# A Macaron block on one core: FFN and Mamba cut into steps and woven by a written order

## The chip, the cores and the metric

The kernel runs on one core of a Trainium2 chip. The metric is the device time of one execution in microseconds. The core has engines that each work through a queue of their own, in order: TensorE (PE, matrix products), VectorE (DVE, elementwise and scans), ScalarE (ACT, activation functions, each from a table that must be loaded), GpSimd (POOL), and SyncE (SP), which here issues the transfers (DMA). An engine waits for another by semaphores.

## The reference, cut to what matters

Four sequences of 512 tokens and 128 features pass through two Macaron blocks. The first is half an FFN, a Mamba layer, half an FFN; the second is half a mixture of experts, attention, half a mixture of experts. The change concerns the first one:

```python
# FFN on layernorm(x), 128 -> 512 -> 512 -> 512 -> 128
h = silu(x @ w1) * (x @ w2)
h = gelu(h @ h1)
h = gelu(h @ h2)
return h @ w3
# Mamba on layernorm(x); 256 inner channels, 16 states
x_ssm, z = split(x @ in_proj)
xc = silu(causal_conv(x_ssm, 4 taps) + conv_b)
dt_r, B, C = split(xc @ x_proj)              # 1, 16, 16 columns
dt = softplus(dt_r @ dt_proj + dt_proj_b)
h_t = exp(dt * A) * h_(t-1) + dt * B * xc    # for every channel and state
y = sum_n(h * C) + xc * D
return y * silu(z) @ out_proj
# x = x + FFN(x)/2;  x = x + Mamba(x);  x = x + FFN(x)/2
```

All is computed in float32.

## The kernel before, in words

Activations lie with the features across the 128 partitions and the 512 tokens of a sequence (here called a block, 0 to 3; x0 to x3) along a row. `first_half` treats the first Macaron block, `second_half` the mixture of experts and attention.

`ffn` makes two 512 wide products into one PSUM tile `pair` (two buffers). The first layer has 8 matmuls, a Silu (L244) and a gate product (L245); each of the two hidden layers has 16 matmuls (L227) in two halves with a Gelu after each half (L251); the last has 4 (L255) and an add into x (L257).

`mamba_first` is everything ahead of the scan: layernorm (L186 to L202), the products with in_w (L271, L276), the convolution on VectorE (L281, L283), Silu, the row of dt apart from the rows of B and C (L291, L293), dt's softplus from Exp and Ln (L319 to L330). B and C go to DRAM and come back broadcast over 32 partitions each (L300, L306), in a pool of three buffers. `mamba_spread` (L337) copies 32 channels of dt and of dt*xc four times over the partitions: tile `rep`, four of them per block, k = 0 to 3.

The scan of a block has 16 steps, 8 in each of two halves. A step is two Exps that make `da` (L349, three buffers), a product with B (L351), two scans (L353) and a product with C (L354) on VectorE, and two narrow matmuls that sum over states into `acc` (L361). `mamba_last` adds the skip term (L371), makes y (L375), multiplies by out_w (L379) and adds into x (L380).

In `first_half` FFN 0 and `mamba_first` of block 0 come first. Then for each block: the first half of the scan, one FFN (in block 0 FFN 1 ahead of the scan and FFN 2 and 3 in the middle; later the second FFN of the block before), `mamba_first` of the next block, the second half of the scan, `mamba_last`. The second FFN of block 3 comes after all this, beside the first routing of the experts.

This text is not the order on the engines. A scheduler at build time puts every instruction into its engine's queue by the order of the text, by its own estimates of durations and by priority: what stands under `with early()` counts as standing 3000 places ahead. In the queue the order is then fixed. `wait_for` makes an instruction wait for another's end, `ln_exp` loads a table once an instruction is done.

Of the kernel before, what the change touches and what calls it, by code (L numbers as in the profile page):

```python
# [29 lines left out]
P = 128  # L30
# [13 lines left out]
EARLY = 3000  # L44
EPS = 1e-5
# [10 lines left out]
def macaron(ctx: ExitStack, tc: tile.TileContext, a: dict, out: bass.AP):  # L56
# [161 lines left out]
    def ffn(pool, pair, b):  # L218


        def product(w, h, c, n):

            ps = pair.tile([P, 2, S], F32, tag="pair", name="pair")
            for i in range(2):
                cut = slice((2 * c + i) * P, (2 * c + i + 1) * P)
                for k in range(n):
                    nc.tensor.matmul(  # L227
                        ps[:, i, :],
                        lhsT=w[:, cut] if n == 1 else w[:, k, cut],
                        rhs=h if n == 1 else h[:, k, :],  # L230
                        start=k == 0,
                        stop=k == n - 1,
                    )
            return ps

        with early():
            xn = layernorm(b)
        h = pool.tile([P, NH, S], F32, tag="h", name="h")
        for c in range(NH // 2):
            p1 = product(w1, xn, c, 1)  # L240
            p2 = product(w2, xn, c, 1)
            g = pool.tile([P, 2, S], F32, tag="g", name="g", bufs=1)
            with early():
                nc.scalar.activation(g, p1, AF.Silu)  # L244
                nc.vector.tensor_mul(h[:, 2 * c : 2 * c + 2, :], p2, g)  # L245
        for w in (h1, h2):
            nxt = pool.tile([P, NH, S], F32, tag="h", name="hn")
            for c in range(NH // 2):
                ps = product(w, h, c, NH)
                with early():  # L250
                    nc.scalar.activation(nxt[:, 2 * c : 2 * c + 2, :], ps, AF.Gelu)  # L251
            h = nxt
        ps = pair.tile([P, 2, S], F32, tag="pair", name="pair")[:, 0, :]
        for k in range(NH):
            nc.tensor.matmul(ps, lhsT=w3[:, k, :], rhs=h[:, k, :], start=k == 0, stop=k == NH - 1)  # L255
        with early():
            nc.vector.tensor_add(xs[b], ps, xs[b])  # L257

# [3 lines left out]
    def mamba_first(pool, b):  # L262
        with early():
            xn = layernorm(b)
        xi = pool.tile([P, NC, S + DCONV - 1], F32, tag="xi", name="xi", bufs=1)
        nc.gpsimd.memset(xi[:, :, 0 : DCONV - 1], 0.0)
        z = pool.tile([P, NC, S], F32, tag="z", name="z")
        for c in range(NC):
            ps = aux()
            with early():  # L270
                nc.tensor.matmul(ps, lhsT=in_w[:, c * P : (c + 1) * P], rhs=xn, start=True, stop=True)  # L271
            nc.scalar.copy(xi[:, c, DCONV - 1 :], ps)
        for c in range(NC):
            ps = aux()
            with early():
                nc.tensor.matmul(ps, lhsT=in_w[:, DI + c * P : DI + (c + 1) * P], rhs=xn, start=True, stop=True)  # L276
            nc.scalar.activation(z[:, c, :], ps, AF.Silu)
        xc = pool.tile([P, NC, S], F32, tag="xc", name="xc")
        for c in range(NC):
            cv = pool.tile([P, S], F32, tag="cv", name="cv")  # L280
            nc.vector.tensor_scalar_mul(cv, xi[:, c, 0:S], col(V_CW + c * DCONV))  # L281
            for k in range(1, DCONV):
                nc.vector.scalar_tensor_tensor(  # L283
                    cv, xi[:, c, k : k + S], col(V_CW + c * DCONV + k), cv, ALU.mult, ALU.add
                )
            nc.scalar.activation(xc[:, c, :], cv, AF.Silu, bias=col(V_CB + c))
        ps_r = aux(1)
        ps_bc = aux(2 * NST)
        with early():
            for k in range(NC):  # L290
                nc.tensor.matmul(ps_r, lhsT=xp_w[:, k, 0:1], rhs=xc[:, k, :], start=k == 0, stop=k == NC - 1)  # L291
            for k in range(NC):
                nc.tensor.matmul(ps_bc, lhsT=xp_w[:, k, 1:], rhs=xc[:, k, :], start=k == 0, stop=k == NC - 1)  # L293
        rank = pool.tile([1, S], F32, tag="rank", name="rank", bufs=1)
        nc.scalar.copy(rank, ps_r)
        bc = pool.tile([2 * NST, S], F32, tag="bc", name="bc", bufs=1)
        nc.scalar.copy(bc, ps_bc)

        rows = dram.tile([2 * NST, S], F32, tag="rows", name="rows")
        nc.sync.dma_start(out=rows, in_=bc)  # L300
        bcs = []
        for i, name in enumerate(("B", "C")):
            t = pool.tile([P, NQ, S], F32, tag="bcs", name=name, bufs=3)
            for m in range(NM):
# [3 lines left out]
                    in_=rows[lo : lo + NQ].rearrange("q t -> (q t)").partition_broadcast(R),  # L308
                )
            bcs.append(t)  # L310

        both = pool.tile([P, 2, NC, S], F32, tag="both", name="both", bufs=1)
        dt, dx = both[:, 0], both[:, 1]
        e = pool.tile([P, NC, S], F32, tag="e", name="e", bufs=1)
        for c in range(NC):
            ps = aux()
            with early():
                last = nc.tensor.matmul(ps, lhsT=dt_w[:, c * P : (c + 1) * P], rhs=rank, start=True, stop=True)
            nc.scalar.activation(e[:, c, :], ps, AF.Abs, bias=col(V_DTB + c))  # L319
            nc.scalar.activation(dt[:, c, :], ps, AF.Relu, bias=col(V_DTB + c))  # L320
        u = pool.tile([P, NC, S], F32, tag="u", name="u", bufs=1)
        table = ln_exp(last)
        first = nc.scalar.activation(e, e, AF.Exp, scale=-1.0)
        after(table, first)
        nc.scalar.activation(dx, e, AF.Ln, bias=1.0)
        nc.vector.tensor_scalar(u, e, 1.0, 1.0, ALU.add, ALU.subtract)
        nc.vector.tensor_sub(u, e, u)
        nc.vector.tensor_add(u, u, dx)
        nc.vector.tensor_add(dt, dt, u)
        nc.vector.tensor_mul(dx, dt, xc)  # L330
        return z, xc, bcs, both

    def mamba_spread(pool, both, k):

        t = pool.tile([P, 2, NC, S], F32, tag="rep", name="rep", bufs=4)
        for m in range(NM):
            nc.sync.dma_start(out=t[m * R : (m + 1) * R], in_=both[k * R : (k + 1) * R])  # L337
        return t

    def mamba_half(pool, made, ys, half):  # L340
        z, xc, (bs, cs), both = made
        ks = (2 * half, 2 * half + 1)
        reps = [mamba_spread(pool, both, k) for k in ks]
        for q in range(NQ):
            sums = []
            for k, t in zip(ks, reps):
                da = pool.tile([P, NC, S], F32, tag="da", name="da", bufs=3)
                for c in range(NC):
                    nc.scalar.activation(da[:, c, :], t[:, 0, c, :], AF.Exp, scale=neg_a[:, k, c, q : q + 1])  # L349
                h = pool.tile([P, NC, S], F32, tag="hs", name="hs", bufs=4)  # L350
                nc.vector.tensor_mul(h, t[:, 1], bs[:, q].unsqueeze(1).to_broadcast([P, NC, S]))  # L351
                for c in range(NC):
                    nc.vector.tensor_tensor_scan(h[:, c, :], da[:, c, :], h[:, c, :], 0.0, ALU.mult, ALU.add)  # L353
                nc.vector.tensor_mul(h, h, cs[:, q].unsqueeze(1).to_broadcast([P, NC, S]))  # L354
                sums.append((k, h))

            with early():
                for k, h in sums:
                    for c in range(NC):
                        at = (k + 2 * c) % 4 * R  # L360
                        nc.tensor.matmul(  # L361
                            ys[c][at : at + R, :], lhsT=sum4, rhs=h[:, c, :], start=q == 0, stop=False,
                            skip_group_check=True,
                        )

    def mamba_last(pool, b, made, ys):
        z, xc, _, _ = made
        y = pool.tile([P, NC, S], F32, tag="e", name="y", bufs=1)
# [5 lines left out]
        for c in range(NC):  # L374
            nc.vector.tensor_mul(y[:, c, :], z[:, c, :], ys[c])  # L375
        with early():
# [3 lines left out]
        nc.vector.tensor_add(xs[b], xs[b], ps)  # L380

    def first_half(fpool, pair):


        with tc.tile_pool(name="mamba", bufs=2) as pool:
            ffn(fpool, pair, 0)
            made = mamba_first(pool, 0)
            for b in range(NB):
                now = made
                if b == 0:  # L390
                    ffn(fpool, pair, 1)
                ys = [acc() for _ in range(NC)]
                mamba_half(pool, now, ys, 0)
                if b == 0:
                    ffn(fpool, pair, 2)
                    ffn(fpool, pair, 3)
                else:
                    ffn(fpool, pair, b - 1)
                if b + 1 < NB:
                    made = mamba_first(pool, b + 1)  # L400
                mamba_half(pool, now, ys, 1)
                mamba_last(pool, b, now, ys)
# [401 lines left out]
```

## Time and profile before

| | us |
|---|---|
| median of 3 runs | 1862.45 (1861.93 to 1862.87) |
| profiled execution | 1863.84 |
| its span, first to last instruction | 1862.1 |
| first half, to x3 out of Mamba | 0 to 564.2 |
| last FFN, experts and attention | 564.2 to 1862 |
| TensorE busy in the whole span | 1737.3 |
| VectorE busy in the whole span | 1122.8 |
| ScalarE busy in the whole span | 814.8 |
| mean granted clock of TensorE | 0.972 |

The page cuts the span into 40 slices of 46.6 us; each digit is the busy share in tenths. A row of a stage table gives, for a stretch of the span, the busy time of each engine with the number of its instructions, the granted clock of TensorE (1.00 is full speed), the busy share of the transfer engines and what they moved. A row of waits reads: engine, what it was about to do and its line, what it waited for, us in total, how many times, the longest. A row of the timeline reads: start, length, engine, line, operation, what it writes and reads, how many in sequence, and in brackets the idle time ahead of it and what ended that. A float32 matmul is recorded as two passes, so x32 are 16 matmuls.

### The profile page before, as it was taken

How to read it: one execution, taken by the hardware profiler on the slowest of the kernel's cores; microseconds unless marked ns; L12 is line 12 of the kernel's file. 1: busy time of each engine (PE TensorE's matmuls, PEld its weight loads, DVE VectorE, ACT ScalarE, POOL GpSimd, SP SyncE). 2: the span in 40 equal slices, each digit the busy share in tenths (PEclk: the TensorE clock that was granted, in tenths of full speed). 3: DMA queues.
4: the chain of work that ended last, by engine and by line, in shares of the span. 5: the costliest groups of instructions: out<-in, count | busy, mean ns of one | idle time of the engine just before them, and what ended most of it. 6: DMA issues, size and time to landing. Idle time of an engine off the chain costs nothing.

```text
span 1862.1 us, 13356 instructions
## 1 busy us (share of the span) xinstructions
PE 1737.3 (93%) x4482; PEld 753.0 (40%) x4482; DVE 1122.8 (60%) x1976; ACT 814.8 (44%) x1213; POOL 4.3 (0%) x22
## 2 busy tenths in 40 slices
PE   6899999795949999999999999999999999999999
PEld 3333333231303444444455445544454445444443
DVE  3138969796793555656466556655665566565554
ACT  2357867483623322323444445443544355422222
POOL 0000000000000000000000000000000000000000
PEclk9989999996959999999999999999999999999999
DMA  2060232305006000000000000000000000000000
GB/s 95 5 133 0 59 78 58 79 10 127 1 0 227 1 1 0 0 0 1 0 1 0 1 1 0 1 0 0 1 1 6 1 1 0 6 1 1 6 1 6
DMA packets 14442, 42.28 MB, mean 23 GB/s; under 512 B 5068, under 2 KB 6053, under 8 KB 11045
## 3 DMA queue, kind: packets, MB, share of 16 engines
q1 hardware_dynamic: 14373, 41.43, 8.9%
q8 instruction: 35, 0.57, 0.1%
q14 instruction: 34, 0.28, 0.0%
HBM read 23.33 MB, written 1.31 MB: 13 GB/s over the span
## 4 chain that ended last, share of the span: by engine, by line
PE 72%; DVE 18%; ACT 6%; issue 3%; DMA 1%; SPq 0%; DVEq 0%; ACTq 0%
PE acc L514 16%; PE pair L519 15%; PE pair L520 15%; DVE hs L353 7%; PE pair L227 7%; PE aux L575 4%; PE acc L613 4%; DVE hs L351 3%; DVE hs L354 2%; PE aux L603 2%; PE aux L195 2%; PE aux L560 1%; PE aux L567 1%; ACT L160 1%; PE aux L189 1%
## 5 line engine op out<-in xcount | busy, mean ns | idle before, releaser
L522 ACT ACTIVATE g<-pair 128x512 f32<-128x512 f32 (+1 forms) x368 | 219.7, 597 | 639.6 <-PE pair L520 638.3
L525 DVE TENSOR_TENSOR gr<-g,rw 128x512 f32<-128x512 f32 x352 | 242.7, 690 | 338.7 <-ACT g L522 338.7
L514 PE MATMUL acc<-h,wd 128*128 128x512 f32 x704 | 362.4, 596 | 8.7 <-DVE h L528 8.7
L519 PE MATMUL pair<-xn,wg 128*128 128x512 f32 x704 | 359.9, 593 | 0.0
L520 PE MATMUL pair<-xn,wu 128*128 128x512 f32 x704 | 359.5, 592 | 0.0
L528 DVE TENSOR_TENSOR h<-gr,pair 128x512 f32<-128x512 f32 x352 | 240.5, 686 | 25.4 <-DVE gr L525 0.9
L514 PEld LDWEIGHTS acc<-h,wd 128*128 128x128 f32 x704 | 128.8, 189 | 175.9 <-DVE h L528 110.7
L520 PEld LDWEIGHTS pair<-xn,wu 128*128 128x128 f32 x704 | 133.4, 190 | 161.4 <-issue 158.8
L519 PEld LDWEIGHTS pair<-xn,wg 128*128 128x128 f32 x704 | 126.3, 190 | 119.9 <-issue 117.2
L353 DVE TENSOR_TENSOR_SCAN hs<-da,hs 128x512 f32<-128x512 f32 x128 | 150.0, 1209 | 29.0 <-ACT da L349 28.8
L361 PE MATMUL acc<-hs,sum 128*32 128x512 f32 x256 | 84.5, 697 | 62.8 <-DVE hs L354 62.8
L227 PE MATMUL pair<-h,h 128*128 128x512 f32 x256 | 117.3, 602 | 2.4 <-ACT g L244 2.3
L227 PE MATMUL pair<-hn,h 128*128 128x512 f32 x256 | 117.5, 601 | 0.0
L349 ACT ACTIVATE da<-rep,neg_a 128x512 f32<-128x512 f32 x128 | 83.9, 712 | 39.2 <-DVE hs L353 38.8
L575 PE MATMUL aux<-kt,q 128*128 128x512 f32 (+3 forms) x256 | 91.4, 441 | 4.1 <-ACT pt L608 2.7
L588 ACT ACTIVATE p<-p,a_low 128x128 f32<-128x128 f32 (+3 forms) x128 | 70.2, 549 | 31.6 <-DVE a_low L577 31.6
L354 DVE TENSOR_TENSOR hs<-hs,C 128x1024 f32<-128x1024 f32 x64 | 77.7, 1214 | 0.2
L351 DVE TENSOR_TENSOR hs<-rep,B 128x1024 f32<-128x1024 f32 x64 | 76.5, 1206 | 1.2 <-PE acc L361 1.2
L613 PE MATMUL acc<-pt,vo 128*128 128x512 f32 (+3 forms) x256 | 76.2, 433 | 0.0
L227 PEld LDWEIGHTS pair<-h,h 128*128 128x128 f32 x256 | 46.6, 190 | 72.2 <-issue 61.4
L227 PEld LDWEIGHTS pair<-hn,h 128*128 128x128 f32 x256 | 46.7, 190 | 69.4 <-issue 65.7
L577 DVE CUSTOM_DVE_ANT_0 p<-aux,mask 128x512 f32<-128x512 f32 (+3 forms) x128 | 62.0, 487 | 21.0 <-PE aux L575 21.0
(149 smaller groups left out, 1504.2 us busy)
## 6 DMA issues: line engine op xcount, KB each, us to landing
rep<-both SPq DMA_DIRECT2D x64, 256.0 KB, 7.3
B<-rows SPq DMA_DIRECT2D x16, 256.0 KB, 4.7
C<-rows SPq DMA_DIRECT2D x16, 256.0 KB, 4.9
h<-in_h SPq DMA_DIRECT2D x2, 1024.0 KB, 9.0
wg<-in_wg SPq DMA_DIRECT2D x4, 384.0 KB, 7.4
wu<-in_wu SPq DMA_DIRECT2D x4, 384.0 KB, 7.4
wd<-in_wd SPq DMA_DIRECT2D x4, 384.0 KB, 7.4
wg<-in_wg SPq DMA_DIRECT2D x4, 320.0 KB, 7.2
```

Source lines behind the costliest of these rows:

```text
L227: nc.tensor.matmul(ps[:, i, :], lhsT=w[:, cut] if n == 1 else w[:, k, cut], rhs=h if n == 1 else h[:, k, :], start=k == 0, stop=k == n - 1,)
L351: nc.vector.tensor_mul(h, t[:, 1], bs[:, q].unsqueeze(1).to_broadcast([P, NC, S]))
L353: nc.vector.tensor_tensor_scan(h[:, c, :], da[:, c, :], h[:, c, :], 0.0, ALU.mult, ALU.add)
L354: nc.vector.tensor_mul(h, h, cs[:, q].unsqueeze(1).to_broadcast([P, NC, S]))
L514: nc.tensor.matmul(po, lhsT=w, rhs=h, start=n == 0, stop=n == len(jobs) - 1)
L519: nc.tensor.matmul(pg, lhsT=wg_, rhs=xn, start=True, stop=True)
L520: nc.tensor.matmul(pu, lhsT=wu_, rhs=xn, start=True, stop=True)
L522: nc.scalar.activation(g, pg, AF.Silu)
L525: nc.vector.tensor_mul(gr, g, rw)
L528: nc.vector.tensor_mul(h, g, pu)
L575: nc.tensor.matmul(sc, lhsT=q[:, i * P : n], rhs=kt[:, 0:n], start=True, stop=True)
L613: nc.tensor.matmul(po[:, j * P :], lhsT=vo[:, j, h, :], rhs=pt[:, lo : lo + n], start=h == 0 and j == 0, stop=h == HEADS - 1 and j == NT - ...
```

## The change

`ffn`, `mamba_first` and the scan become generators that stop after each step: an FFN has 12 steps, `mamba_first` 6, a scan 16 and its end. `first_half` asks for one step after another: FFN 0 with the first step of FFN 1 in it; `mamba_first` of block 0 with two steps of FFN 1 after each of its own; then, in each block, after every scan step as many FFN steps as `FILL` says, and from the fifth scan step on, at every second one, a step of the next block's `mamba_first`. In block 0 these are the rest of FFN 1, and FFN 2 and 3; in blocks 1 to 3 three FFN steps follow three of every four scan steps (the second FFN of the block before).

The tiles rep 0 and 1 of the next block are now filled before the last part of a block, and B and C have four buffers, so that those of two blocks fit. Both Gelus of a layer run one after the other, and the first waits for the last matmul of the layer. dt's row and the rows of B and C come out of one matmul with 33 columns. All of `mamba_first` and the sums and end of a block stand under `early()`. Some tiles share memory under common names (`inner`, `wide`).

```diff
+FILL = ((2, 1) * 7 + (1, 1), *[(0, 1, 1, 1) * 4] * 3)
 def ffn(pool, pair, b):
...
         with early():
             xn = layernorm(b)
+        yield
...
         for w in (h1, h2):
             nxt = pool.tile([P, NH, S], F32, tag="h", name="hn")
+            both = [two(), two()]
             for c in range(NH // 2):
-                ps = product(w, h, c, NH)
-                with early():
-                    nc.scalar.activation(nxt[:, 2 * c : 2 * c + 2, :], ps, AF.Gelu)
+                product(both[c], 0, w, h, c, NH)
+                yield
+                last = product(both[c], 1, w, h, c, NH)
+                if c:
+                    with early():
+                        for i in range(2):
+                            act = nc.scalar.activation(nxt[:, 2 * i : 2 * i + 2, :], both[i], AF.Gelu)
+                            if not i:
+                                wait_for(last, act)
+                yield
...
 def mamba_first
-                nc.tensor.matmul(ps_r, lhsT=xp_w[:, k, 0:1], rhs=xc[:, k, :], start=k == 0, stop=k == NC - 1)
-            for k in range(NC):
-                nc.tensor.matmul(ps_bc, lhsT=xp_w[:, k, 1:], rhs=xc[:, k, :], start=k == 0, stop=k == NC - 1)
+                nc.tensor.matmul(ps, lhsT=xp_w[:, k, :], rhs=xc[:, k, :], start=k == 0, stop=k == NC - 1)
+            nc.scalar.copy(rows, ps)
...
-            t = pool.tile([P, NQ, S], F32, tag="bcs", name=name, bufs=3)
+            t = pool.tile([P, NQ, S], F32, tag="bcs", name=name, bufs=4)
...
 def first_half
-            ffn(fpool, pair, 0)
-            made = mamba_first(pool, 0)
...
+            STEPS = 12
+            order = [f for b in range(1, NB) for f in [before_[b]] * STEPS]
+            second = [ffn(fpool, pair, b) for b in range(NB - 1)]
+            order += [f for f in second for _ in range(STEPS)]
...
+            go(before_[0], 4)
+            filler(1)
+            go(before_[0], STEPS - 4)
+            first = mamba_first(pool, 0, made)
+            for _ in first:
+                filler(2)
             for b in range(NB):
-                now = made
+                rest = mamba_rest(pool, b, made)
                 if b == 0:
-                    ffn(fpool, pair, 1)
-                ys = [acc() for _ in range(NC)]
-                mamba_half(pool, now, ys, 0)
...
+                    mamba_spread(pool, 0, made, 0)
+                    mamba_spread(pool, 0, made, 1)
+                mamba_spread(pool, b, made, 2)
+                mamba_spread(pool, b, made, 3)
+                nxt = mamba_first(pool, b + 1, made) if b + 1 < NB else iter(())
+                for step in range(4 * NQ):
+                    go(rest)
+                    if step >= 4 and step % 2 == 0:
+                        go(nxt)
+                    filler(FILL[b][step])
                 if b + 1 < NB:
-                    made = mamba_first(pool, b + 1)
-                mamba_half(pool, now, ys, 1)
-                mamba_last(pool, b, now, ys)
+                    mamba_spread(pool, b + 1, made, 0)
+                    mamba_spread(pool, b + 1, made, 1)
+                go(rest)
```

## The prediction

> **What bounds the kernel now.** I read the page first, then a table of busy time by stage, then the waits of VectorE, then single stretches of the timeline.
>
> ```profile
> span 1862.1 us, 13356 instructions
> PE 1737.3 (93%) x4482; PEld 753.0 (40%) x4482; DVE 1122.8 (60%) x1976; ACT 814.8 (44%) x1213; POOL 4.3 (0%) x22
> ...
> PE   6899999795949999999999999999999999999999
> ...
> DVE  3138969796793555656466556655665566565554
> ...
> PEclk9989999996959999999999999999999999999999
> ```
>
> The averages mislead: from slice 14 on (the second half, which the change does not touch) TensorE is full. The digits below 9 lie in the first 12 slices, and there VectorE is the one at 9.
>
> ```profile
> core 0: us, PE busy (x) PEld busy (x) DVE busy (x) ACT busy (x) POOL busy (x), PEclk, DMA share, GB/s
> 70.00:153.00 83.00, 70.96 (x146) 27.48 (x146) 30.09 (x35) 44.53 (x51) 0.10 (x1) 0.88 0.37 77
> 153.00:244.00 91.00, 82.81 (x205) 26.61 (x203) 80.83 (x78) 67.09 (x77) 0.10 (x1) 1.00 0.27 57
> 244.00:353.00 109.00, 98.12 (x237) 32.33 (x236) 93.54 (x92) 72.29 (x85) 0.10 (x1) 0.97 0.30 63
> 353.00:455.00 102.00, 79.42 (x188) 23.88 (x188) 86.36 (x85) 65.20 (x77) 0.00 (x0) 0.90 0.23 50
> 455.00:564.20 109.20, 75.75 (x164) 22.04 (x164) 79.46 (x73) 43.23 (x52) 0.57 (x2) 0.77 0.09 19
> 564.20:1862.00 1297.80, 1274.35 (x3420) 594.10 (x3420) 737.02 (x1585) 506.41 (x856) 2.38 (x8) 1.00 0.03 9
> ```
>
> The cuts are the moments at which Mamba has finished a block (x0 at 244, x1 at 353, x2 at 455, x3 at 564.2). Everything after 564.2 hangs on x3 and takes 1297.8. So the question is when x3 is ready. VectorE is idle 15.5, 15.6 and 29.7 us in the last three blocks, TensorE more, ScalarE most: VectorE's queue sets the pace, with holes. From the first steady scans at 158.6 to its last C product's end at 554.8 it is busy 334.3 of 396.2 us, idle 61.9. What it waits for there:
>
> ```profile
> DVE xn L201 <- ACT rs L199: 15.0, 6, 5.5
> DVE y L375 <- PE acc L371: 12.1, 6, 4.0
> DVE h L245 <- PE pair L227: 10.2, 3, 6.1
> DVE xm L191 <- PE aux L189: 9.1, 5, 2.7
> DVE hs L353 <- ACT da L349: 8.5, 3, 3.9
> ```
>
> The first four are the seam between two blocks: sums, y, out_w, layernorm, gate of the next FFN, one after another with no scan to put between. Why there is none shows in SP's queue:
>
> ```profile
> 222.54 0.51 SPq L337 DMA_DIRECT2D rep<-both  x1
> 225.88 1.69 SPq L306 DMA_DIRECT2D C<-rows  x4
> 227.62 17.33 SPq L337 DMA_DIRECT2D rep<-both  x15
> ```
>
> C of block 1 stood until a third buffer came free at block 0's last B product, and 15 rep transfers stood behind it.
>
> **The steady price.** Without disturbance a step (B product, two scans, C product) takes 4.50 us of VectorE:
>
> ```profile
> 519.74 2.33 DVE L353 TENSOR_TENSOR_SCAN hs<-da,hs 128x512 f32<-128x512 f32 x2
> 519.87 1.92 PE L361 MATMUL acc<-hs,sum 128*32 128x512 f32 x4 [4.05 <-DVE hs L354]
> ...
> 524.24 2.33 DVE L353 TENSOR_TENSOR_SCAN hs<-da,hs 128x512 f32<-128x512 f32 x2
> ```
>
> that is 1.13 an instruction when they follow each other. A 512 wide matmul is 0.86 (16 of them from 113.12 to 126.96).
>
> **The change, in stages.** I laid the recorded order of the new program, queue by queue, over these durations.
>
> *To x0 (FFN 0).* The layernorm of x1 moves into FFN 0: 2 matmuls, +1.7. Both Gelus of a layer now wait for its last matmul, so TensorE stands while the first runs: about 0.2 + 1.02 + 0.1, 1.35 a layer, twice. x0 at 75 against 70.75.
>
> *To x1.* TensorE does FFN 1 (44 matmuls), in_w 4, xp 2, dt 2, two layernorms 4: 56 x 0.86 = 48. The waits inside Mamba's first part (its convolution, the two aux buffers, which copies free) I put at 4, the Gelu waits at 2.7: x1 at 129, before 146.2 (17 earlier, since mamba_first(0) no longer runs on a standing TensorE). B and C in one matmul with dt's row: 2 matmuls and a 0.57 copy fewer per block; the slack that TensorE and ScalarE have in every later stage hides it, and at the start it is inside the 48.
>
> *To steady scans.* Here it loses again. mamba_first(1) is now asked for from step 4, and stands in ScalarE's queue ahead of the da that scans 2 and 3 need. From x1 ScalarE's queue holds 12 table loads (15.4) and 25 activations (17), with some 6 of waits: steady scans at 168, two steps and six B products done. Before: 158.6.
>
> *To the y of block 0.* VectorE's queue from there: 30 scans, 11 B and 15 C products at 1.13 (63), u and dt of block 1 5.5, two gates 2.3, one add 0.6: 72, with the first step of block 1 in it. 241; before 239.4. TensorE needs some 65 in it and does not bind.
>
> *Blocks 1 to 3.* VectorE's work by count: 87 + 90 + 78.5 = 255.6. Its waits: at seam 0/1 a scan stands between the last sum and y, so y waits for nothing; what stays is out_w (1.2), the mean (1.2), the second mean (1.6), 2 for da. 6 in all. At seam 1/2 no scan stands there in the new order: y 4.5, 1.2, 1.2, then the gate of the next FFN (4 matmuls, Silu's table load, Silu) 5.7, and 2 where the dx of block 3 waits behind a pair of Gelus: 14.6. At seam 2/3 one B product lies before y and two scans before out_w: 3.5, mean 0.7, layernorm's table load, Ln and Exp 5.5, gate 1.8: 11.5. Together 32, where before some 56 of waiting lay between the y of block 0 and 554.8. Last C product's end: 241 + 255.6 + 32 = 528.6. From there 9.4 to x3, as 554.8 to 564.2: x3 at 538, **26.2 earlier**.
>
> *The rest.* In the last FFN nothing is woven in, so 2 x 1.35 of Gelu waits appear; the new order puts four transposes (0.6) and one layernorm (1.7), which before stood after it, into these waits: +0.4. Transfers: bufs 4 for B and C let C go at once; rep 0 and 1 of the next block are issued at half a block. A block's rep takes 17.3 to 18.9 us of issue, and the first half it serves lasts 8 x 4.5 = 36, so that they cost nothing; were this cover gone, one rep would be 5 to 7 us at a seam. The rows, B and C of the block after next stand in SP's queue behind rep 2 and 3, which wait for buffers that come free at a block's end; the rows are made only some five steps later. The shared names `inner` and `wide` order xi, e and y, and cv and u, one after another, as the computation does anyhow: nothing. Sum on the span: -25.8. The profiled execution itself was 1863.84, 1.7 above its span, and the median of the runs 1862.45; I take the difference over to it: **1837**.
>
> **Two rules against rows.** (1) The row: through the lonely scans of block 3 (516 to 552) the granted clock is 0.54 and a pair of sums takes 1.92, with pauses of only 2.58 us; the same pair in the full stretch takes 1.05. The Trainium skill ("TensorE: Matmul & The Clock Gate", "Why this matters for your kernels") says that only pauses over some 3 us throttle. It bears on this change, which spreads TensorE's work thinner: the new order still ends block 2 with six sums and block 3 with three with nothing between. By the rule these seams would be warm, y about 2 us sooner at each, x3 at 534; by the row they are as cold as before. I take the row. Where three matmuls lie between sums, TensorE has 3.5 of 4.5 us to do and both say warm. (2) The same skill's "ScalarE: Activation LUTs" ("What ACT_TABLE_LOAD costs") asks 2.66 us for a switch, drain included; here the load at 472.32 is followed by its da at 473.61, 1.29 later. The new order has 82 loads where there were 101 before the second half's first sigmoid: 24 us of ScalarE by the row, 51 by the rule. It was busy at most 72 of 109, so neither is on the path; but by the rule the 12 loads ahead of the steady scans would cost 17 more, and x3 would come at 555.
>
> **Rivals.** *The weave fills more* (I took the order of the queues as strict at every place where two of them meet): the gate waits, the da and dx waits and half the y waits go, 17 us; 1820. For it: within a block VectorE already ran 46.0 of 46 us at 280 to 326. Against: layernorm and out_w are true chains, and the new order leaves them bare at two seams.
> *The start costs more*: if mamba_first(1) holds steady scans back to 180 rather than 168, 12 of 26 are gone: 1849. For it: the two queues wait for each other there (da behind Silu behind convolution behind scans).
> *Slower: a pair of Gelus at the head of ScalarE's queue.* It now waits for the whole layer, and the da of the next scans stand behind it. 12 pairs lie in the woven stretch; da has three buffers, so a pair that waits up to two steps (9 us) is hidden. In block 3 before, single Gelus that waited 5.9 and 2.5 cost VectorE 3.9 and 3.4 us. At 3.9 a pair it is 47, less the 2 counted: 1882; it decides from 28 / 12 = 2.3 us a pair. Against: the new order puts 10 to 13 da ahead of most pairs.
> *The change does not reach the end*: the transfers were not late, and block 0 ends no earlier; with the waits of the old seams kept, the start's loss of 1.6 and the Gelu waits leave 1862 to 1865.
>
> **How the numbers follow.** My account 0.58 (own range 1825 to 1848, from +-12 on 32 of waits and on the 168); fills more 0.17; start costs more 0.16; no effect 0.04; slower 0.05. 0.2% is 3.7 us, about what a measurement of this kernel can tell from no change. Faster 0.91, same 0.04, slower 0.05. No waits at all in blocks 1 to 3 would be 1805; I cut the range at 1815 below, and above at 1857, where the start has lost 20 of the 26.
>
> **What would show it.** x1 added at 129 and x0 at 75; VectorE steady only from about 168; the y of block 0 near 241; x0, x1, x2 out of Mamba near 244, 338, 446 and x3 at 538; waits of VectorE from the first steady scan to its last C product about half of 61.9; y waiting for nothing at the first seam and 4 at the second; 1298 after x3. I am wrong if scans wait for da for more than 10 us in all, or if x3 comes after 556.

## The result, and the profile after

The changed kernel takes 1835.53 us (median, 1834.04 to 1835.65) against 1862.19 of the kernel before: a ratio of 0.9855, 95% interval 0.9838 to 0.9873. The prediction was 1837, range 1815 to 1857. The profiled execution took 1834.04, its span is 1832.2. It is the fastest of its kernel's four, and the profiled one of the kernel before (1863.84) is above all its other runs; so the two spans differ by 29.9 where the medians differ by 26.7, and a difference of some 3 us between two profiles is not yet an effect.

From the page of the changed kernel: the busy times, and the rows of TensorE, VectorE and the granted clock in 40 slices.

```profile
PE 1717.3 (94%) x4466; PEld 749.4 (41%) x4466; DVE 1123.2 (61%) x1976; ACT 785.3 (43%) x1189; POOL 4.3 (0%) x22
PE   6999899785869999999999999999999999999999
DVE  3127989798963656556566646665566466565554
PEclk9999999997989999999999999999999999999999
```

VectorE does the same work as before (1123 us, 1976 instructions). ScalarE lost 29 us and 24 instructions, most of it table loads; it was never full, and an experiment below gives the loads back. What changed is how tightly VectorE's work lies. The table by stages from x0 on, cut where a block has left Mamba:

```profile
core 0: us, PE busy (x) PEld busy (x) DVE busy (x) ACT busy (x) POOL busy (x), PEclk, DMA share, GB/s
244.65:341.34 96.69, 83.50 (x202) 27.01 (x200) 86.27 (x84) 60.71 (x74) 0.11 (x1) 0.96 0.32 66
341.34:446.75 105.41, 79.77 (x184) 24.66 (x184) 93.13 (x91) 60.34 (x74) 0.00 (x0) 0.87 0.29 61
446.75:532.90 86.15, 66.25 (x164) 20.82 (x164) 75.30 (x69) 39.12 (x48) 0.49 (x2) 0.94 0.00 0
532.90:1832.20 1299.30, 1274.51 (x3420) 594.13 (x3420) 737.08 (x1586) 504.55 (x855) 2.46 (x9) 1.00 0.03 9
```

Blocks 1 to 3 take 96.7, 105.4 and 86.2 us where they took 109.3, 102.1 and 108.7 (from one add into x to the next). The gain of 31 up to x3 (564.2 to 532.9) is made in block 1 (13) and above all in block 3 (23); block 2 is 3 longer, x0 comes 0.6 later, and the part after x3 is 1.5 longer. VectorE's waits from the y of block 0 to the last C product:

```profile
DVE y L394 <- PE acc L390: 7.9, 4, 3.8
DVE h L249 <- ACT g L248: 7.0, 1, 7.0
DVE xn L202 <- ACT rs L200: 4.5, 1, 4.5
DVE xm L192 <- PE aux L190: 4.2, 3, 1.6
```

With four small rows they are 29.3 us. All that these four show lies at the three seams. What feeds a scan hardly appears: in the whole answer no B product or scan waits for a transfer or for `da`.

### The profile page after: what moved, and what is told of

Read it like the earlier page. It is cut to its first block, busy times and chain, and to the rows that moved or that the text cites. A ratio compares the mean times of both kernels' runs of the same rounds, so it can differ in the third digit from the quotient of the medians.

```text
span 1832.2 us, 13288 instructions
## 1 busy us (share of the span) xinstructions
PE 1717.3 (94%) x4466; PEld 749.4 (41%) x4466; DVE 1123.2 (61%) x1976; ACT 785.3 (43%) x1189; POOL 4.3 (0%) x22
## 4 chain that ended last, share of the span: by engine, by line
PE 72%; DVE 17%; ACT 7%; issue 3%; DMA 0%; SPq 0%; DVEq 0%; ACTq 0%
PE acc L559 16%; PE pair L565 16%; PE pair L564 16%; DVE hs L376 7%; PE pair L225 6%; PE aux L620 4%; PE acc L658 4%; DVE hs L374 3%; DVE hs L377 2%; PE aux L648 2%; PE aux L605 2%; PE aux L612 2%; PE aux L196 1%; PE aux L190 1%; PE pair L268 1%
## 5 line engine op out<-in xcount | busy, mean ns | idle before, releaser
L382 PE MATMUL acc<-hs,sum 128*32 128x512 f32 x256 | 75.6, 672 | 53.3 <-DVE hs L377 52.9
L620 PE MATMUL aux<-kt,q 128*128 128x512 f32 (+3 forms) x256 | 91.4, 441 | 4.1 <-ACT pt L653 2.7
L225 PE MATMUL pair<-xn,w 128*128 128x512 f32 x128 | 65.1, 646 | 10.9 <-DVE xn L202 7.1
```

Of the source, the lines that this page charges most:

```text
L225: m = nc.tensor.matmul(ps[:, i, :], lhsT=w[:, cut] if n == 1 else w[:, k, cut], rhs=h if n == 1 else h[:, k, :], start=k == 0, stop=k == n ...
L620: nc.tensor.matmul(sc, lhsT=q[:, i * P : n], rhs=kt[:, 0:n], start=True, stop=True)
```

## Experiments

Each kernel was timed against the kernel before on its chip; that kernel's medians lay between 1861.3 and 1862.8, so that the ratios can be compared with one another.

### The Gelus of a layer apart again

```diff
-                last = product(both[c], 1, w, h, c, NH)
-                if c:
-                    with early():
-                        for i in range(2):
-                            act = nc.scalar.activation(nxt[:, 2 * i : 2 * i + 2, :], both[i], AF.Gelu)
-                            if not i:
-                                wait_for(last, act)
+                product(both[c], 1, w, h, c, NH)
+                with early():
+                    nc.scalar.activation(nxt[:, 2 * c : 2 * c + 2, :], both[c], AF.Gelu)
```

> The changed kernel with one part undone: a Gelu runs as soon as its own half of the layer is there, and nothing waits for the layer's last matmul. My account (the gain is VectorE's waits at the seams of blocks): the two waits of 1.35 us per FFN go where nothing else runs (FFN 0, FFN 1, the last FFN), and ScalarE gets some 20 table loads more, which are off the path: 1832 to 1838. Rival (fewer table loads are the gain): most of the 26 us is lost, 1855 or more.

Measured: 1832.14 (1831.34 to 1832.62), ratio 0.9842 [0.9827, 0.9856]. TensorE's waits in FFN 0 of the changed kernel have these rows, which the kernel with Gelus apart does not have:

```profile
PE pair L225 <- ACT hn L261: 1.1, 1, 1.1
PE pair L268 <- ACT hn L261: 1.1, 1, 1.1
```

x0 is added at 71.15 instead of 74.25 and x1 at 122.28 instead of 129.48, but x3 comes at 533.02 instead of 532.25: the whole gain at the start is spent again at the seams, whose order came out differently (blocks of 109.4, 90.9 and 91.5). The part after x3, where the last FFN stands unwoven, is 2.5 shorter (1297.5 from the add into x to the end, instead of 1300.0); but in six of the seven kernels below that keep the Gelus paired it lies between 1298.0 and 1299.5 (two steps ahead of y aside), so most of that is scatter. Running the Gelus together, and with it the fewer table loads, is no source of the gain. That it costs some 3 us is not shown: the two intervals overlap.

### Three buffers for B and C, and rep asked for late

```diff
-            t = pool.tile([P, NQ, S], F32, tag="bcs", name=name, bufs=4)
+            t = pool.tile([P, NQ, S], F32, tag="bcs", name=name, bufs=3)
...
-                if b + 1 < NB:
-                    mamba_spread(pool, b + 1, made, 0)
-                    mamba_spread(pool, b + 1, made, 1)
                 go(rest)
+                if b + 1 < NB:
+                    mamba_spread(pool, b + 1, made, 0)
+                    mamba_spread(pool, b + 1, made, 1)
```

> The changed kernel with one part undone: B and C in three buffers, and rep 0 and 1 of the next block asked for after a block's end. My account: C stands in SP's queue until the block's last B product, rep 0 lands some 10 us after that, and the scan that could stand in a seam waits for it: 5 to 8 us at each of three seams, 1850 to 1860, with VectorE waiting for transfers. Rival (the transfers were not late before, so bringing them forward is worth nothing): 1834 to 1838.

Measured: 1832.54 (1830.86 to 1832.88), ratio 0.9842 [0.9828, 0.9857]. My expectation failed. Undoing the transfers costs nothing, although the order at the seams came out differently here too (blocks of 87.0, 103.4 and 95.2). SP's queue of this kernel at the end of block 0:

```profile
191.41 36.01 SPq L359 DMA_DIRECT2D rep<-both  x9
231.38 1.70 SPq L321 DMA_DIRECT2D C<-kept  x4
```

C is as late as it was before, but it now stands behind nine rep transfers and not ahead of fifteen. Where rep is asked for in the text made no difference: here it begins at 191.41, after the last product into `both` (the tile of dt and dt*xc that rep copies) at 190.15, and in the changed kernel at 191.57 after 190.31. In both kernels `both` is early. So the question became what makes `both` early.

### The next block's preparation without priority

In `mamba_first` only the matmuls and the layernorm stay under `early()`, as they did in the kernel before; its copies, convolution, Silus and softplus take their place by the text.

```diff
-        with early():
-            for c in range(NC):
-                ps = aux()
+        for c in range(NC):
+            ps = aux()
+            with early():
                 nc.tensor.matmul(ps, lhsT=in_w[:, c * P : (c + 1) * P], rhs=xn, start=True, stop=True)
-                nc.scalar.copy(xi[:, c, DCONV - 1 :], ps)
+            nc.scalar.copy(xi[:, c, DCONV - 1 :], ps)
...
-        with early():
-            for c in range(NC):
-                nc.vector.tensor_scalar_mul(cv[:, c, :], xi[:, c, 0:S], col(V_CW + c * DCONV))
+        if True:
+            for c in range(NC):
+                nc.vector.tensor_scalar_mul(cv[:, c, :], xi[:, c, 0:S], col(V_CW + c * DCONV))
...
-        with early():
+        if True:
             table = ln_exp(last)
```

> The changed kernel with one part undone: in the part of Mamba ahead of the scan only the matmuls (and the layernorm) stand ahead of the text's order, as before the change, and ScalarE's and VectorE's instructions there do not. My account (this part of the next block stands in front of the da of block 0's second and third scans and delays steady scans from 158 to 168): steady scans some 8 us sooner, and as nothing else moves, 1826 to 1830. Rival (the priority pays, since the next block is then ready at each seam): slower than the changed kernel, 1840 to 1850.

Measured: 1847.29 (1847.1 to 1847.71), ratio 0.9924 [0.9909, 0.9939]. My expectation failed again, the other one held. SP's queue of this kernel at the end of block 0, then VectorE's waits from the y of block 0 to the last C product:

```profile
231.78 18.78 SPq L361 DMA_DIRECT2D rep<-both  x16
```

```profile
DVE y L396 <- PE acc L392: 10.4, 6, 4.0
DVE xn L202 <- ACT rs L200: 9.7, 5, 4.5
DVE xm L192 <- PE aux L190: 9.5, 5, 3.1
```

Block 0 does end 8 us sooner (x0 at 235.83 instead of 243.96), as I had said. But the last product into `both` of the next block now comes at 230.49, 333.00 and 438.01, each only some five to ten us before the block ends, instead of 190.31, 303.97 and 399.56. At each seam the next block's first B product comes only after a layernorm (244.30, 351.13, 455.78), y and the layernorms wait bare (xn and xm 9.7 and 9.5 us; in the changed kernel 4.5 and 4.2), and the blocks take 107.2, 105.0 and 98.8. 8 won at the start, 22.7 lost in blocks 1 to 3, 1.4 won after x3: 13 on the span. The priority of the preparation is worth some 12 of the 27 us. The kernel before with this priority alone was not run, so how the other 15 divide among the parts is not shown.

### The transfers alone, in the kernel before

First both of them in the old text (B and C with four buffers, the shared names that make room for these, and rep 0 and 1 asked for ahead of `mamba_last`):

```diff
-            t = pool.tile([P, NQ, S], F32, tag="bcs", name=name, bufs=3)
+            t = pool.tile([P, NQ, S], F32, tag="bcs", name=name, bufs=4)
...
                 mamba_half(pool, now, ys, 1)
+                if b + 1 < NB:
+                    reps = [mamba_spread(pool, made[3], k) for k in (0, 1)]
                 mamba_last(pool, b, now, ys)
```

> The kernel before with one part of the change alone: B and C in four buffers (with the shared names that make room for them), and rep 0 and 1 of the next block asked for ahead of a block's end. No weaving, Gelus apart. My account: scans of the next block can stand in the seams, which held some 45 us of VectorE's waits before; without the weave the order uses only part of it: 8 to 15 us, 1847 to 1854. Rival (the weave does it): 1860 to 1863.

Measured: 1843.09 (1842.13 to 1843.65), ratio 0.9899 [0.9883, 0.9916]; 4 us better than the best that I had expected. Then the buffers and shared names alone, without the `reps` lines:

> The kernel before with B and C in four buffers and the shared names alone: rep is asked for where it was. It tells what part of before_ahead (1843.1) did it. If C standing in SP's queue ahead of 15 rep transfers was the harm, C now goes at once and nearly all of that gain is here: 1842 to 1848. If rep asked for sooner in the text was it: 1857 to 1862.

Measured: 1845.96 (1842.32 to 1848.36), ratio 0.9911 [0.9895, 0.9927]. Nearly all of it is block 3, 91.4 instead of 108.7. Its transfers, in the kernel before and then in this one:

```profile
435.34 1.15 SPq L337 DMA_DIRECT2D rep<-both  x2
442.04 1.70 SPq L306 DMA_DIRECT2D C<-rows  x4
443.79 16.09 SPq L337 DMA_DIRECT2D rep<-both  x14
```

```profile
394.46 1.76 SPq L307 DMA_DIRECT2D C<-rows  x4
413.68 30.32 SPq L338 DMA_DIRECT2D rep<-both  x16
```

The eight transfers of rep 0 and 1, which the first steps need, are issued by 422.2 instead of 449.9 (the other eight of the last row wait until 435.65). Of these 28 us some 7 are C's stand in the queue (436.49 to 443.79). The other 22 are an earlier `both` (412.40 instead of 434.06): with a buffer free, the scheduler ordered the whole preparation of block 3 sooner. At the seam a step of block 3 now lies around the layernorm's first operation (VectorE, this kernel):

```profile
452.96 1.22 DVE L352 TENSOR_TENSOR hs<-rep,B 128x1024 f32<-128x1024 f32 x1
454.26 0.69 DVE L191 TENSOR_TENSOR xm<-x,aux 128x512 f32<-128x512 f32 x1
454.87 2.33 DVE L354 TENSOR_TENSOR_SCAN hs<-da,hs 128x512 f32<-128x512 f32 x2
```

So the buffers, with rep asked for sooner or not, are worth 17 to 18 us in the kernel before; taken back together with rep's place they cost nothing in the changed one. Two parts of the change, the buffers and the priority, reach the same thing, the next block's steps ready before the seam; their gains do not add.

### One step of the next block ordered ahead of y

If bare seams are the cost, a step that stands ahead of y by order must gain. One step of the next block (its sums later, in their old place) is ordered before each y of the block; two in a second kernel.

```diff
+                    for k in range(1):
+                        ahead[b + 1, k, 0] = mamba_step(pool, b + 1, made, k, 0)
                 go(rest)
...
-                nc.vector.tensor_mul(y[:, c, :], z[:, c, :], ys[c])
+                then = nc.vector.tensor_mul(y[:, c, :], z[:, c, :], ys[c])
+                if b + 1 < NB:
+                    after(made[b + 1][4]['done'], then)
```

> The changed kernel with one scan step of the next block (its sums left for later) put ahead of each y, by an order on VectorE. My account: the bare y waits at seams 1/2 (4.0) and 2/3 (3.9) are filled: 5 to 8 us, 1827 to 1831. Rival (a wait that is filled there comes back later, since what follows a seam, layernorm and gate, starts that much later): 1833 to 1837.

Measured: 1817.34 (1816.64 to 1818.24), ratio 0.976 [0.9744, 0.9777]: 18 us below the changed kernel, where 5 to 8 were expected. VectorE at seam 2/3, in the changed kernel and then in this one:

```profile
441.52 0.69 DVE L394 TENSOR_TENSOR y<-z,acc 128x512 f32<-128x512 f32 x1 [2.88 <-PE acc L390]
443.23 0.69 DVE L394 TENSOR_TENSOR y<-z,acc 128x512 f32<-128x512 f32 x1 [1.02 <-PE acc L390]
```

```profile
428.06 1.22 DVE L370 TENSOR_TENSOR hs<-rep,B 128x1024 f32<-128x1024 f32 x1
429.38 2.34 DVE L372 TENSOR_TENSOR_SCAN hs<-da,hs 128x512 f32<-128x512 f32 x2
431.75 1.23 DVE L373 TENSOR_TENSOR hs<-hs,C 128x1024 f32<-128x1024 f32 x1
432.90 1.32 DVE L400 TENSOR_TENSOR y<-z,acc 128x512 f32<-128x512 f32 x2
```

y waits for nothing at seams 1/2 and 2/3 either. From the y of block 0 to the last C product VectorE is busy 254.0 of 271.3 us, in the changed kernel 254.6 of 284.6: 13 us, all waits. y's 7.9 are gone as expected. The gate's 7.0 at seam 1/2 are gone too, and that I had not expected: one order given changed the places of the others, and why the gate's place changed was not followed up. The other waits are some 2 longer. The rest lies before block 0's y (0.8), in the chain after the last C product (1.4) and after x3 (2.0).

> As forced1 with two steps ahead of each y. My account: the second step fills the waits for out_w and the mean too where the order uses it, but puts the end of a block 4.5 us later for TensorE: 1825 to 1832. Rival: the later start of layernorm and FFN costs more than it fills: 1836 to 1842.

Two steps: 1833.97 (1833.41 to 1835.81), ratio 0.985 [0.9835, 0.9864]. y again waits for nothing at the three seams, but VectorE now waits ahead of it: 6.2 for the `da` of the added steps at seam 0/1 (the y of block 0 comes at 254.97 instead of 240.41 with one step), and 8.2 and 9.6 at the other two for the last product of an FFN, whose add the order puts there. Two of these rows:

```profile
251.00 2.34 DVE L372 TENSOR_TENSOR_SCAN hs<-da,hs 128x512 f32<-128x512 f32 x2 [6.16 <-ACT da L368]
...
441.00 0.69 DVE L270 TENSOR_TENSOR x<-pair,x 128x512 f32<-128x512 f32 x1 [9.59 <-PE pair L268]
```

x3 comes at 528.66, 12 us later than with one step and 3.6 earlier than in the changed kernel, but 5 us more than there lie after it; that last part was not followed up. With one step nothing new waits ahead of y; with two, such waits came in.

### TensorE kept at work ahead of a seam

Fifteen matmuls with zero weights, three after each of scan steps 11 to 15 of block 2, add zeros to a sum that is being made; the sum stays what it is. (Counted from 0, as in the code and the expectation, these are steps 10 to 14.)

```diff
+                        if b == 2 and 10 <= (half * NQ + q) * 2 + k % 2 < 15:
+                            for _ in range(3):
+                                nc.tensor.matmul(
+                                    ys[0], lhsT=none, rhs=h[:, 0, :], start=False, stop=False, skip_group_check=True
+                                )
```

> The changed kernel with 15 matmuls added that add zeros to a sum (3 after each of steps 10 to 14 of block 2, where TensorE has nothing but two narrow matmuls per 4.5 us); the output is the same. By the row (such stretches are cold, 0.54 granted): granted clock 1.0 at the end of block 2, y of that seam waits 2.5 us less, out_w, layernorm and the first layer of the next FFN run at full speed, 3 to 5 us in all: 1830 to 1833. By the rule that only pauses over some 3 us throttle: nothing changes, 1835.

Measured: 1832.66 (1831.97 to 1833.04), ratio 0.9841 [0.9826, 0.9855]. The stretch ahead of seam 2/3 and the seam, in the changed kernel and then in this one:

```profile
410.00:440.00 30.00, 15.00 (x35) 2.79 (x36) 28.61 (x26) 6.75 (x11) 0.00 (x0) 0.66 0.42 85
440.00:447.00 7.00, 5.38 (x9) 1.87 (x8) 4.46 (x6) 0.00 (x0) 0.00 (x0) 0.74 0.00 0
```

```profile
410.00:440.00 30.00, 24.99 (x64) 7.75 (x64) 28.94 (x27) 7.25 (x11) 0.00 (x0) 0.94 0.39 79
440.00:447.00 7.00, 5.64 (x17) 1.75 (x14) 5.81 (x7) 0.00 (x0) 0.00 (x0) 1.00 0.19 37
```

The granted clock rises from 0.66 to 0.94 and from 0.74 to 1.00, and y's waits fall from 3.9 to 0.2:

```profile
441.58 0.69 DVE L402 TENSOR_TENSOR y<-z,acc 128x512 f32<-128x512 f32 x1
442.44 0.69 DVE L402 TENSOR_TENSOR y<-z,acc 128x512 f32<-128x512 f32 x1 [0.17 <-PE acc L398]
```

Not all of that is the clock: VectorE also reaches the seam 1.6 us later in this kernel, and a scan stands ahead of y. From the end of the block's last C product to the second y it is 3.3 us (439.13 to 442.44) instead of 5.7 (437.50 to 443.23); these 2.4 are what the clock can claim, and the expectation had 2.5. So that more work on TensorE brings the clock back is shown. A gain in the total is not: the interval overlaps the changed kernel's, and in the profiles block 2 is 1.5 shorter, but x3 comes no sooner (532.36, 532.25 in the changed kernel), and the 1.3 that lie after it this edit does not touch.

### Other places for the FFN steps

```diff
-FILL = ((2, 1) * 7 + (1, 1), *[(0, 1, 1, 1) * 4] * 3)
+FILL = ((2, 1) * 7 + (1, 1), *[(0,) * 7 + (12,) + (0,) * 8] * 3)
```

> Edit: in blocks 1 to 3 the twelve FFN steps all stand after the eighth scan step, as one FFN stood between the two halves before; the rest of the change stays. The order of the queues differs from the changed kernel's in block 1 to 3, since the scheduler still moves FFN products into free places of TensorE's queue. My account (VectorE's queue and its seams set the end, the even places of FFN steps are of little worth by themselves): 1831 to 1840, TensorE busy as before in every block. Rival (the even weave is the gain: without it TensorE's work bunches up in the middle and y and the gates wait at the seams): 1845 to 1858, VectorE's waits in blocks 1 to 3 back to 45 us or more.

Measured: 1827.71 (1825.16 to 1828.12), ratio 0.981 [0.9796, 0.9825], 8 us faster than the even weave. Neither theory had that; the one that says evenness is the gain is the further off. At seam 1/2, where in the changed kernel y stands bare, the order happened to put work of the next block (VectorE of this kernel):

```profile
339.99 0.69 DVE L394 TENSOR_TENSOR y<-z,acc 128x512 f32<-128x512 f32 x1 [0.47 <-PE acc L390]
340.59 1.22 DVE L376 TENSOR_TENSOR_SCAN hs<-da,hs 128x512 f32<-128x512 f32 x1
341.73 0.66 DVE L394 TENSOR_TENSOR y<-z,acc 128x512 f32<-128x512 f32 x1
```

With one FFN step after each of the first twelve scan steps (`(1,) * 12 + (0,) * 4`):

> Edit: in blocks 1 to 3 one FFN step after each of the first twelve scan steps and none after the last four, instead of three after every four. The queues of VectorE, ScalarE and the transfers come out unchanged, TensorE's differs in a few neighbours. My account (the scheduler places the work, the text's places count only where they change its order): 1834 to 1837, no difference from the changed kernel. Rival (evenness of the places counts): 1842 or more.

1834.74 (1833.18 to 1836.19), ratio 0.985 [0.9834, 0.9867]: no difference. VectorE runs the same order as in the changed kernel, and yet x3 comes 2.3 later in this profile (534.51): that much is scatter between executions.

### The improvements put together

> Edit: both earlier improvements in one kernel, one scan step of the next block ordered ahead of y (1817.3 alone) and each Gelu right after its own half of a layer (1832.1 alone, 3.4 less than the changed kernel). If the two gains are in different places, the Gelu's at the start and in the last FFN, the other's at the seams, they add up: 1812 to 1816. If the orders that the scheduler makes at the seams are what moved in both, they don't: 1816 to 1830.

One step ahead of y and the Gelus apart: 1815.2 (1814.84 to 1815.54), ratio 0.9746 [0.9732, 0.9761]. It is the fastest kernel here, 1.1% below the changed one. The time is in the range expected for gains that add up; but what the Gelus add to the ordered step, 2.1 us, lies within overlapping intervals.

> Edit: one scan step of the next block ahead of y, each Gelu after its own half (together 1815.2), and the twelve FFN steps of blocks 1 to 3 all after the eighth scan step (1827.7 alone, where by chance two scans, a B and a C product of the next block came to lie beside y and the add at one seam). If what the places of the FFN steps gained was that work at the seam, an ordered step makes it superfluous: 1812 to 1818. If the bunched FFN steps gain something of their own in the middle of the blocks: 1804 to 1810.

The same with FFN steps in the middle: 1823.28 (1820.73 to 1824.37), ratio 0.9789 [0.9773, 0.9805]; 8 slower than without, which no expectation covered. At seam 2/3 an FFN's add (L266, 3.2 us of waiting) has come to stand ahead of y, y follows at 438.93, and the add into x2 waits 3.3 for the product with out_w, 1.2 in the kernel above (VectorE of this kernel):

```profile
435.93 0.69 DVE L266 TENSOR_TENSOR x<-pair,x 128x512 f32<-128x512 f32 x1 [3.17 <-PE pair L264]
443.49 0.69 DVE L402 TENSOR_TENSOR x<-x,aux 128x512 f32<-128x512 f32 x1 [3.28 <-PE aux L401]
```

x2 comes 5.8 us later by it than in the kernel above, x3 8. Moving the FFN steps to the middle gained 8 in one surrounding and lost 8 in another: what it changes is which instruction happens to stand at a seam, and I have no rule for it.

## Why the prediction was right, and where it was not

**The sum.** Its parts beside what was measured:

| step | predicted | measured |
|---|---|---|
| x0 added by FFN 0 | 75 | 74.94 |
| x1 | 129 | 130.2 |
| steady scans from | 168 | 169.2 |
| y of block 0, without a wait | 241 | 241.2 |
| VectorE's work to the last C product | 255.6 | 254.6 |
| its waits, seams 0/1, 1/2, 2/3 | 6, 14.6, 11.5 | 6.5, 13.4, 9.4 |
| last C product ends | 528.6 | 525.8 |
| from there to x3 | 9.4 | 7.1 |
| x3 | 538 | 532.9 |
| after x3 | 1298.2 | 1299.3 |
| span | 1836.3 | 1832.2 |

(The waits by seam are summed from the single rows of VectorE's timeline; together they are the 29.3 of all its waits. Two sums of the prediction are off in the last digit: 168 and 72 are 240, not 241, and the three counts of work make 255.5, not 255.6.) The account held because every instruction's place in the recorded order was used with durations from the trace. The largest wait was foreseen in kind: 5.7 for the gate of the next FFN at seam 1/2, behind Silu's table load, and it was 7.0. At seam 0/1 the agreement is partly luck: the 2 for `da` never came, and a B product and two operations of an FFN waited 2.0 in their place. The 2 for dx at seam 1/2 did not come either. Off in size were the chain behind the last C product (2.3 too long) and seam 2/3 (2.1). For the last FFN "+0.4" was 1.5, which is within the scatter of the part after x3. The agreement of 538 with 532.9 is that of one profile, the fastest; by the medians the change gained 26.7 where 25.8 was forecast.

**The step that failed** is the reason given for the bare seams: "C of block 1 stood until a third buffer came free at block 0's last B product, and 15 rep transfers stood behind it", and with it "bufs 4 for B and C let C go at once" as what helps. For the kernel before it is half the reason: the buffer is worth 17 us there, but of the 28 by which block 3's first transfers came forward, 22 are an earlier `both` and only 7 C's stand. And one of its three seams was not bare. At seam 1/2 of the kernel before, a step of block 2 already stood around y:

```profile
344.69 2.33 DVE L353 TENSOR_TENSOR_SCAN hs<-da,hs 128x512 f32<-128x512 f32 x2
348.75 0.69 DVE L375 TENSOR_TENSOR y<-z,acc 128x512 f32<-128x512 f32 x1 [1.73 <-PE acc L371]
...
358.63 1.22 DVE L354 TENSOR_TENSOR hs<-hs,C 128x1024 f32<-128x1024 f32 x1
```

The C product of these scans comes after y, so they are the next block's. In the changed kernel the buffer's worth does not show. There the early `both` comes from the priority of `mamba_first`, which I had booked as a loss alone ("Here it loses again", steady scans held back). The loss is real, 8 us; the same edit brings 22.7 later. The numbers came out right because the recorded order contained its effect, whichever edit had made it: the forecast of the time is sound, the reason given for it was wrong in part.

**The rules against the rows.** The clock: the row was right, the seam was granted 0.74 and y waited 3.9. But the seam did not test the two against each other. The Trainium skill ("TensorE: Matmul & The Clock Gate", "Why this matters for your kernels") asks for no pause over some 3 us; that only such pauses throttle is the prediction's reading. And a pause of 4.05 us stands at the head of the cold stretch, in the kernel before (519.87, in the prediction's own lines) and in the changed one (420.55, below), so the page's row had no reason to call these seams warm; the added matmuls took that pause away too. What speaks against "only" are cold pairs elsewhere that no pause over 3 us precedes; they stand in the last section. The table load: a load at 353.89 is followed by its Silu at 355.19, 1.30 later, so the price of the row held against the 2.66 of "ScalarE: Activation LUTs" ("What ACT_TABLE_LOAD costs"): the load itself, 1.28 here, agrees with that section, the drain does not show. Steady scans came at 169.2, where the rule would have put them 17 later.

**The rivals.** The weave did not fill more by itself, but "1820" was about the size for an order with more of the waits gone: 1817.3 with one step ahead of y. The start cost what was predicted. Pairs of Gelus at the head of ScalarE's queue cost VectorE nothing (no wait for `da` stands in its rows after 241); they cost TensorE 1.1 each in FFN 0, where little is woven in. That evenness of the weave is what helps is not supported: the uneven kernels were 8 faster and equal.

What stays open: why one order of the seams comes out of the scheduler and not another. Kernels here differ by 8 us by that alone (the FFN steps in the middle); differences of 3 are near the scatter.

## What to carry to other kernels

Where one engine's queue sets the time, look at the places where a chain of dependent operations crosses engines with nothing between, and put one independent piece of work ahead of the chain by an explicit order; one step gained 18 us here, of which 8 are the chain that it covers and 7 a wait elsewhere that went with the new order; with two steps the gain was gone, to new waits that the order put ahead of the chain. Preparing the next block early looks like a loss in the block where it is done and pays at the seam, so an edit of this kind is costed over both. And two edits that each bring the same work forward don't add: test each alone in the old kernel as well as undone in the new one.

## What the runs showed of the hardware

TensorE's clock stays low, and at times falls, although it pauses only briefly. Its timeline in the changed kernel, from the last stretch of block 2:

```profile
415.45 1.05 PE L382 MATMUL acc<-hs,sum 128*32 128x512 f32 x4 [0.68 <-DVE hs L377]
420.55 1.92 PE L382 MATMUL acc<-hs,sum 128*32 128x512 f32 x4 [4.05 <-DVE hs L377]
...
434.05 1.92 PE L382 MATMUL acc<-hs,sum 128*32 128x512 f32 x4 [2.58 <-DVE hs L377]
```

After one pause of 4.05 the pair of sums takes 1.92 instead of 1.05, and it still does 14 us later, when all pauses since were 2.58. Fifteen matmuls that add zeros, which made TensorE busy 25.0 instead of 15.0 of 30 us, kept the clock at 0.94 there.

Shorter pauses were enough elsewhere. The first row is of the kernel with the added matmuls, just ahead of them, the second of the kernel with the Gelus apart, at the end of block 3:

```profile
411.46 1.92 PE L385 MATMUL acc<-hs,sum 128*32 128x512 f32 x4 [1.92 <-DVE hs L380]
```

```profile
511.80 1.92 PE L378 MATMUL acc<-hs,sum 128*32 128x512 f32 x4 [2.91 <-DVE hs L373]
```

In the 20 us before each of them no pause was longer; the granted clock was 0.51 from 411.4 to 413.4 in the first and 0.52 from 510 to 527 in the second. In the changed kernel the same pause of 1.92, ahead of 410.95, left the pair at 1.05 and the clock at 1.00. So in these traces the length of a pause alone does not decide whether the clock falls; what does is left open.
